# The start of an SSD layer: the first batch's norm made in place and in skewed stages, the first front beside it, and two kinds of stores on ScalarE's queue

## The chip, the cores and the metric

The kernel runs on one core of a Trainium2 chip. The metric is device time in microseconds for one execution of the whole program. Engines are named as in the profile: PE (TensorE; PEld are its weight loads), DVE (VectorE), ACT (ScalarE), POOL (GpSimd), and SP (SyncE), which issues DMAs.

## What is computed

Four layers follow each other on an image batch of 4 x 96 x 64 x 64 in f32: a selective-scan layer with a fusion and a batch norm, a state-space layer with scalar decays (the "SSD" layer), the first kind again, and a ConvNeXt block. The change touches the second layer alone. Cut to what matters, with L = 64 x 64 tokens, 3 heads of 64, 128 states:

```python
residual = x                                   # [4, 96, L]
xn = rmsnorm over the 96 channels of x, times norm_w
xs = xn in four orders: rows, rows reversed, columns, columns reversed
z, xBC, dt = split(xs @ in_proj_w.T)           # 192, 192 + 2 * 128, 3 columns
dt = softplus(dt + dt_bias)
xBC = silu(causal convolution of xBC over 4 tokens + conv_b)
y = ssd(x, dt, -exp(A_log), B, C) + D * x      # within chunks and from chunk to chunk
y = rmsnorm(y * silu(z)) @ out_proj_w.T
out = mean of the four orders, put back in place, + residual
```

The layer's x is not stored by the layer before. That layer leaves its raw output (raw), its residual (res) and the scale and shift of its batch norm (bn), which are known only when its last token is done. So the SSD layer first makes x = raw * scale + shift + res, "the sum".

## The kernel before

Class Ssd holds the layer. A batch is 96 channels by 4096 tokens. Three sizes of pieces occur: chunks of T = 512 tokens (NT = 8) in the preparation, blocks of BLK = 1024 tokens in the front, and chunks of Q = 128 tokens in the recurrence, eight (QB) to a block. There are 64 steps, (batch b, order o, direction r, block), four blocks to a direction; o = 0 is by rows, o = 1 by columns, r = 1 reversed.

For each direction there is a prelude (line 763 on). For r = 0 it makes the normalised tokens and the step sizes, for both directions the decays:

- rmsnorm(b) (line 665): for each of the 8 chunks, loads raw and res into the tiles nx and nr (two buffers each), applies the batch norm on ACT (line 673), adds res on DVE (674), stores the sum to DRAM from SP's queue (675), squares on ACT (677), takes the mean over channels by a matmul with a constant matrix (679), makes the inverse root by Ln and Exp on ACT (the helper at line 107), and writes xn[0] on DVE (682).
- turn() (line 684) copies xn[0] into xn[1] by columns, on POOL, for o = 1.
- step_sizes(o) (line 696): for each chunk a matmul into a bank "front" (706), a copy on ACT to a row tile dtrow (711, which shares the two buffers of nsq), a store of it to DRAM from SP's queue (712); then one load of all rows in another layout (717), the softplus on ACT, DVE and POOL, and a transpose on PE (725).
- decays(r) (line 729): cumulative sums by matmuls with triangles (743, 745), exponentials, a transpose (756), and a store of the sums (760), which the steps load again as dr (850), broadcast to all partitions.

weights_of (line 616) loads the layer's weights: inw (620), the convolution's weights conv (624), which DVE multiplies with inw (626) and seven DMAs spread into sconv (629); xbias, bcbias (631, 633); ad (638), of which ACT makes a; the output weights opw and gn (656, 657), multiplied on DVE (659).

front(b, o, r, blk) (line 781) prepares one block: six DMAs stack shifted tokens into pk (777); z by matmuls (796, r = 0 only); B and C by 12 matmuls of pk with sconv (814); x by 24 (825); then one silu over all of it on ACT, which needs another table set (line 112), and transposes of B (842). decay, weights, outputs, scale, by_channels and finish then work on the 128-token chunks, spread over the loop in run() with lags, while front makes the next block and a prelude, taken one step per chunk, the next direction. finish adds the outputs into X (973), a tile that holds the batch's whole sum; switch(b) (line 975) stores X when a batch is done and loads the next batch's sum from DRAM into it (983).

All matmuls of preludes and front go through PSUM banks with the tag "front", of which there are two.

What sets the order: the Python code writes one program, and a planner at build time distributes it over the engines' queues. The place in the program is an instruction's rank; an instruction that is ready by the planner's own durations may go ahead of older ones that are not. The trace shows this: POOL's copies of turn() for o = 1 stand at 3077.30 us, between the chunks of the first norm. Once placed, an engine's queue runs strictly in order, SP's queue of DMAs too. All DMAs of the kernel are issued by SP.

The start of the layer is written out in run():

```python
first = preludes.pop(0)[1]
for _ in range(2):
    next(first)
self.weights_of(self.w)
for _ in first:
    pass
self.switch(0)
for _ in front(0):
    pass
```

That is: two chunks of the first norm, all weights, the rest of the first prelude, the load of X, the first front; then the loop over chunks.

Of the kernel before, what the change touches and what calls it, by code (L numbers as in the profile page):

```python
# [18 lines left out]
F32 = mybir.dt.float32  # L19
AF = mybir.ActivationFunctionType  # L20
ALU = mybir.AluOpType
# [4 lines left out]
B, C, HH, WW = 4, 96, 64, 64  # L26
L = HH * WW
P = 128
T = 512
NT = L // T  # L30
# [27 lines left out]
DI = 192  # L58
DST = 128
NH = 3  # L60
HD = 64
CONV = DI + 2 * DST
# [4 lines left out]
PAD = 3  # L67
# [55 lines left out]
def rsqrt(act, out, in_, eps):  # L123

    act.exp_ln(out, in_, AF.Ln, bias=eps)
    act.exp_ln(out, out, AF.Exp, scale=-0.5)
# [446 lines left out]
class Ssd:  # L573
# [42 lines left out]
    def weights_of(self, w):  # L616

        nc, k, one = self.nc, self.k, self.one
        self.inw = one.tile([C + 1, 2 * DI + 2 * DST + NH], F32, name="inw")
        nc.sync.dma_start(self.inw, w["in"])  # L620

        conv = self.work.tile([P, 3 * BLK], F32, tag="pk", name="conv")
        conv = conv[:C, : 4 * CONV].rearrange("c (k n) -> c k n", k=4)
        nc.sync.dma_start(conv, w["conv_wT"].partition_broadcast(C))
        xbc = self.inw[:C, DI : DI + CONV]
        nc.vector.tensor_tensor(conv, conv, xbc[:, None].to_broadcast([C, 4, CONV]), ALU.mult)
        self.conv = one.tile([P, 3, CONV], F32, name="sconv")
        for i, r0, r1, tap, c0 in PIECES:
            nc.sync.dma_start(self.conv[r0:r1, i], conv[c0 : c0 + r1 - r0, tap])
        self.xbias = one.tile([P, DI], F32, name="xbias")  # L630
        nc.sync.dma_start(self.xbias, w["in"][C, DI : 2 * DI].partition_broadcast(P))
        self.bcbias = one.tile([P, 2], F32, name="bcbias")
        nc.sync.dma_start(
            self.bcbias, w["in"][C, 2 * DI : 2 * DI + 2 * DST].rearrange("(q p) -> p q", q=2)
        )

        self.ad = one.tile([P, 2, NH], F32, name="ad")
        nc.sync.dma_start(self.ad, w["ad"].partition_broadcast(P))
        self.a = one.tile([P, 1, NH], F32, name="a")
        k.act.exp_ln(self.a[:, 0], self.ad[:, 0], AF.Exp)  # L640
        nc.vector.tensor_scalar_mul(self.a, self.a, -1.0)

        self.opw = one.tile([P, 4, C], F32, name="opw")
        gn = one.tile([P, 4], F32, name="gn")
        nc.vector.memset(self.opw, 0.0)
        nc.vector.memset(gn, 0.0)  # L650
        low, up = slice(0, HD), slice(HD, P)
        for j, rows, n, of in (
            (0, slice(0, P), slice(0, P), 0), (1, low, low, 1), (2, up, low, 0), (3, low, up, 0),
            (3, up, up, 2),
        ):
            nc.sync.dma_start(self.opw[rows, j], w["out"][n, of])
            nc.sync.dma_start(gn[rows, j : j + 1], w["gnorm"][n, of : of + 1])
        for j in range(4):
            nc.vector.tensor_scalar(
                self.opw[:, j], self.opw[:, j], gn[:, j : j + 1], 0.25, ALU.mult, ALU.mult  # L660
            )

    def bank(self, tag):
        return self.psum.tile([P, T], F32, tag=tag, name=tag, bufs=2)

    def rmsnorm(self, b):
        nc, k = self.nc, self.k
        for c in range(NT):
            t = ds(c * T, T)
            x, res = (self.work.tile([C, T], F32, name=n) for n in ("nx", "nr"))  # L670
            nc.sync.dma_start(x, self.raw[b, :, t])
            nc.sync.dma_start(res, self.res[b, :, t])
            nc.scalar.activation(x, x, AF.Identity, bias=self.bn[1], scale=self.bn[0])
            nc.vector.tensor_tensor(x, x, res, ALU.add)
            nc.sync.dma_start(self.src[b, :, t], x)
            sq = self.work.tile([C, T], F32, name="nsq")
            nc.scalar.activation(sq, x, AF.Square)
            pv = self.bank("front")[:C]
            nc.tensor.matmul(pv, lhsT=k.mean, rhs=sq, start=True, stop=True)
            rsqrt(k.act, sq, pv, self.eps)  # L680
            xn = self.xn[0][:C, ds(PAD + c * T, T)]
            nc.vector.scalar_tensor_tensor(xn, x, self.norm, sq, ALU.mult, ALU.mult)
            yield

    def turn(self):
# [7 lines left out]
            )  # L693
            yield

    def step_sizes(self, o):

        nc, k = self.nc, self.k
        n = NQ * NH
        rows = self.dram.tile([NH, L], F32, name="dtrows")
        for c in range(NT):
            pd = self.bank("front")[:NH]
            nc.tensor.matmul(
                pd, lhsT=self.inw[:, DI + CONV :], rhs=self.xn[o][:, ds(PAD + c * T, T)],
                start=True, stop=True,
            )
            row = self.work.tile([C, T], F32, tag="nsq", name="dtrow")[:NH]  # L710
            nc.scalar.copy(row, pd)
            nc.sync.dma_start(rows[:, ds(c * T, T)], row)
            yield
        x, ua, lg = (
            self.work.tile([n, Q], F32, tag=m, name=m, bufs=1) for m in ("dtx", "ua", "row")
        )
        nc.sync.dma_start(x, rows.rearrange("h (c t) -> c h t", t=Q))
        yield
        nc.scalar.activation(ua, x, AF.Abs)
        nc.vector.tensor_scalar_max(x, x, 0.0)  # L720
        lo = self.work.tile([C, T], F32, tag="nsq", name="lo")[:n, :Q]
        softplus_tail(nc, k.act, x, ua, lg, lo)
        yield
        pt = self.bank("front")[:, :n]
        nc.tensor.transpose(pt, x, k.ident[:n, :n])
        self.dt = self.work.tile([P, n], F32, name="dt")
        nc.vector.tensor_copy(self.dt, pt)
# [35 lines left out]
    def prelude(self, b, o, r):  # L763

        if r == 0:
            yield from self.rmsnorm(b) if o == 0 else self.turn()
            yield from self.step_sizes(o)
        self.seq[b, o, r] = self.decays(r)

    def stack(self, o, r, blk):  # L770
# [9 lines left out]
    def front(self, b, o, r, blk, made, following):  # L780
# [2 lines left out]


        nc, k = self.nc, self.k
        made.update(self.seq[b, o, r])
        xn = self.xn[o]
        base = blk * BLK
        pk = self.stack(o, r, blk) if self.pk is None else self.pk
# [1 line left out]
        if r == 0:  # L791
            z = self.z[blk] = self.work.tile([P, QB, DI], F32, name="z", bufs=L // BLK + 1)
            for c in range(0, QB, 2):
                p = self.bank("front")[:, : 2 * DI]
                for i in range(2):
                    nc.tensor.matmul(
                        p[:, i * DI : (i + 1) * DI],
                        lhsT=xn[:C, ds(PAD + base + (c + i) * Q, Q)], rhs=self.inw[:C, :DI],
                        start=True, stop=True,
# [8 lines left out]
        x = made["x"] = pre[:, :n1].rearrange("p (c n) -> p c n", c=QB)  # L808
# [177 lines left out]
    def run(self):  # L986
# [16 lines left out]
        def front(n):  # L1003
            if n >= len(steps):
                return iter(())
            return self.front(*steps[n], made[n], steps[n + 1] if n + 1 < len(steps) else None)
# [3 lines left out]
            (n, self.prelude(*steps[n][:3])) for n in range(0, len(steps), nblk)  # L1010
        ]
        first = preludes.pop(0)[1]
        for _ in range(2):
            next(first)
        self.weights_of(self.w)
        for _ in first:
            pass
        self.switch(0)
        for _ in front(0):
            pass  # L1020
        for n in range(-4, len(chunks) + 4):
            def at(lag):
# [289 lines left out]
```

## Time and profile before

| | |
|---|---|
| median of 3 runs | 9949.42 us (9938.72 to 9961.11) |
| the profiled execution | 9940.69 us |
| its span | 9939.0 us |
| busy: PE, DVE, ACT, POOL | 8555.7, 8200.3, 5528.2, 6968.8 us |
| first load of the sum's parts, SSD layer | 3066.55 us |
| first silu's table load in it | 3170.66 us |
| last add into X (line 973) | 6182.87 us |

A row of the order of time reads: start and length in us, engine, line of the kernel, operation, the tile written and the tiles read, how many, and in brackets how long the engine stood idle before it and what ended that. "SPq" is an instruction in SP's queue; its length is that of the issue, and the transfer lands later. Busy time of an engine does not say that it bounds anything; in a start-up stretch in which the engines take turns, all of them are idle most of the time.

### The profile page before, as it was taken

The page shows a single profiled execution, that of the slowest core. Times are in us where ns is not written, and L with a number is a line of the kernel's source. Part 1 is how long each engine was busy: PE and PEld are TensorE (multiplying, and loading weights), DVE is VectorE, ACT ScalarE, POOL GpSimd, SP SyncE. Part 2 cuts the span into 40 slices and gives each one's busy share as a digit, 9 for nine tenths or more (in the row PEclk, how much of TensorE's full clock was granted, in tenths as well). Part 3 has the DMA queues.
Part 4 walks back from the last instruction along what each step waited for, and adds up shares of the span by engine and source line. Part 5 has one row for each costly group of instructions (what it writes and reads, how often), then busy time and mean ns, then how long its engine had stood idle before and what let it go on. Part 6 is the DMA issues. An engine that isn't in the chain of part 4 may idle for free. (4 is left out here: it accounts for less than half of the span.)

```text
span 9939.0 us, 109693 instructions
## 1 busy us (share of the span) xinstructions
PE 8555.7 (86%) x32744; PEld 3519.5 (35%) x32744; DVE 8200.3 (83%) x10861; ACT 5528.2 (56%) x10500; POOL 6968.8 (70%) x4600
## 2 busy tenths in 40 slices
PE   7888888888886998998998988788888888888688
PEld 1222212222212676776776776122222222211122
DVE  7999999999995666666666666799999999999787
ACT  5666666566663455555455554566666665665244
POOL 6888888888884555555555555688888888888322
PEclk8999999999997999999999998899999999999798
DMA  7677677677674223222222222767777777776432
GB/s 189 199 204 202 201 207 206 196 205 208 198 206 121 66 71 92 72 69 83 79 74 74 82 67 57 194 199 205 211 204 206 206 203 200 208 203 199 113 97 74
DMA packets 803535, 1528.27 MB, mean 154 GB/s; under 512 B 124253, under 2 KB 128249, under 8 KB 802170
## 3 DMA queue, kind: packets, MB, share of 16 engines
q1 hardware_dynamic: 802938, 1521.25, 54.4%
q8 instruction: 260, 4.26, 0.2%
q14 instruction: 337, 2.76, 0.1%
HBM read 1229.69 MB, written 156.37 MB: 139 GB/s over the span
## 5 line engine op out<-in xcount | busy, mean ns | idle before, releaser
L342 POOL TENSOR_TENSOR hc<-hs,bc 128x1024 f32<-128x1024 f32 x1536 | 3608.0, 2356 | 630.3 <-DVE hs L340 550.9
L340 DVE TENSOR_TENSOR_SCAN hs<-da,carry,bs 128x512 f32<-128x512 f32 x2016 | 2467.0, 1265 | 81.1 <-DVE bs L335 2.7
L107 ACT ACTIVATE da<-da,w_a 128x512 f32<-128x512 f32 x2304 | 1617.2, 716 | 1273.2 <-DMA da<-dd 1229.1
L361 PE MATMUL py<-hc,selsum 128*32 128x512 f32 x6144 | 1797.4, 637 | 469.8 <-POOL hc L342 463.4
L313 PE MATMUL bs<-du,seldu 64*128 64x512 f32 x4608 | 1570.6, 676 | 208.8 <-DVE hs L340 193.0
L335 DVE TENSOR_TENSOR bs<-bs,bc 128x1024 f32<-128x1024 f32 x1152 | 1398.4, 1214 | 180.2 <-PE bs L313 177.3
L308 POOL TENSOR_TENSOR du<-du,bc 128x1024 f32<-128x1024 f32 x384 | 904.7, 2356 | 279.8 <-DMA du<-dg 144.0
L361 PEld LDWEIGHTS py<-hc,selsum 128*32 128x32 f32 x6144 | 239.3, 110 | 1814.3 <-POOL hc L342 1125.4
L879 POOL TENSOR_TENSOR seg<-seg,cb 128x384 f32<-128x384 f32 x512 | 514.8, 1007 | 516.9 <-DVE cb L878 434.0
L863 DVE TENSOR_SCALAR seg<-dr,dac 128x128 f32<-128x128 f32 x1536 | 645.6, 454 | 276.3 <-PE y L908 269.1
L313 PEld LDWEIGHTS bs<-du,seldu 64*128 64x128 f32 x4608 | 445.6, 195 | 1202.6 <-DVE hs L340 857.0
L194 PE MATMUL pu<-h,w_conv 96*128 96x512 f32 (+3 forms) x2048 | 835.3, 628 | 11.7 <-ACT rs L107 11.6
L340 DVE TENSOR_TENSOR_SCAN hs<-bs,carry,du 128x512 f32<-128x512 f32 x672 | 823.6, 1260 | 6.7 <-issue 5.1
L814 PE MATMUL front<-pk,sconv 128*128 128x512 f32 x1536 | 756.7, 610 | 24.5 <-ACT z L802 20.4
L918 POOL TENSOR_TENSOR y<-y,xs 128x192 f32<-128x192 f32 x496 | 294.4, 594 | 626.0 <-DVE y L917 619.7
L931 ACT ACTIVATE y<-yz 128x192 f32<-128x192 f32 x512 | 186.1, 364 | 903.5 <-DVE yz L930 902.5
L883 POOL TENSOR_TENSOR xs<-pre,coef 128x576 f32<-128x576 f32 x512 | 597.1, 1171 | 65.6 <-ACT pre L112 32.4
L825 PE MATMUL front<-sconv,pk 128*128 128x192 f32 x3072 | 572.8, 329 | 51.1 <-DVE pre L830 46.0
L1175 DVE SCALAR_TENSOR_TENSOR acc<-pad,c_conv,acc 96x1024 f32<-96x1024 f32 x336 | 491.8, 1467 | 110.5 <-ACT acc L1166 59.2
L345 ACT COPY carry<-hs 128x2 f32<-128x2 f32 x1344 | 250.7, 187 | 569.7 <-DVE hs L340 566.1
L825 PEld LDWEIGHTS front<-sconv,pk 128*128 128x128 f32 x3072 | 496.5, 190 | 81.8 <-DVE pre L830 72.3
L107 ACT ACTIVATE bs<-da,w_a 128x512 f32<-128x512 f32 x768 | 522.0, 680 | 2.2 <-DMA da<-dd 0.7
(196 smaller groups left out, 13878.7 us busy)
## 6 DMA issues: line engine op xcount, KB each, us to landing
da<-dd SPq DMA_DIRECT2D x3072, 256.0 KB
du<-dg SPq DMA_DIRECT2D x768, 256.0 KB
dr<-rows SPq DMA_DIRECT2D x256, 384.0 KB
bc<-rows SPq DMA_DIRECT2D x256, 256.0 KB
dd<-delta SPq DMA_DIRECT2D x192, 256.0 KB
dg<-du SPq DMA_DIRECT2D x192, 256.0 KB
pk<-xn SPq DMA_DIRECT2D x128, 384.0 KB
pk<-xn SPq DMA_DIRECT2D x128, 256.0 KB
```

Source lines behind the costliest of these rows:

```text
L107: self.last = self.scalar.activation(out, in_, func, **kw)
L194: nc.tensor.matmul(pu[r0:r1], lhsT=wt["conv"][:kk, tap, d0:d1], rhs=h[:kk, b, ds(tap, T)], start=(tap == 0), stop=(tap == 3),)
L308: nc.gpsimd.tensor_tensor(g["du"], g["du"], self.b_or_c(g, 0), ALU.mult)
L313: nc.tensor.matmul(g["bs"][:, i], lhsT=self.sel["du"][rows, g["half"], g["q"]], rhs=g["made"]["du"][rows, g["j"]], start=True, stop=True,)
L335: nc.vector.tensor_tensor(dbx, dbx, self.b_or_c(g, 0), ALU.mult)
L340: nc.vector.tensor_tensor_scan(hs[:, i], da[:, i], dbx[:, i], init, ALU.mult, ALU.add)
L342: nc.gpsimd.tensor_tensor(g["hc"], hs, self.b_or_c(g, 1), ALU.mult)
L361: nc.tensor.matmul(py[rows], lhsT=self.sel["sum"][:, g["q"]], rhs=g["hc"][:, i], start=(g["q"] == 0), stop=(g["q"] == NQU - 1),)
L814: nc.tensor.matmul(p, lhsT=self.conv[:, i, DI + q * DST : DI + (q + 1) * DST], rhs=pk[:, i, ds(c * T, T)], start=(i == 0), stop=(i == 2),)
L825: nc.tensor.matmul(p, lhsT=pk[:, i, ds(c * Q, Q)], rhs=self.conv[:, i, :DI], start=(i == 0), stop=(i == 2),)
L863: nc.vector.tensor_scalar(seg[:, h], g["pair"]["dr"][:, c % 2 * NH + h], made["dac"][:, n0 + h : n0 + h + 1], 0.0, ALU.subtract, ALU.min,)
L883: nc.gpsimd.tensor_tensor(xs, x.to_broadcast([P, 3, NH, HD]), coef.to_broadcast([P, 3, NH, HD]), ALU.mult)
```

## The change

weights_of becomes a generator with three parts: the loads of inw and conv; the multiplied convolution weights, biases and a; the output weights. The first batch no longer goes through rmsnorm but through a new function, begin(). It loads raw straight into X and res into xn[1], which is free until turn(); two chunks ahead of the first part of the weights, six behind it. Then it makes the sum in X itself, so that neither the store of the sum nor the reload of X is needed for batch 0, and works in stages that are skewed against each other: in turn n the chunk n is summed and squared, n - 1 gets its mean and inverse root, n - 2 its normalised tokens, n - 3 its matmul for the step sizes, and n - 4 its row and the row's store. The squares use the buffers nx and nr by turns. After begin() comes the second part of the weights, then the first front, in which every third step is followed by a step of what is left of the prelude (the load of the rows, the softplus, the transpose and the decays); the output weights come last.

For the other batches rmsnorm loads a chunk one step ahead of its work, and stores the sum from ScalarE's queue, behind the square. The rows of step sizes are stored from ScalarE's queue in all preludes. The diff, without comments and the unchanged rest:

```diff
@@ weights_of
         nc.sync.dma_start(conv, w["conv_wT"].partition_broadcast(C))
+        yield
...
         nc.vector.tensor_scalar_mul(self.a, self.a, -1.0)
+        yield
@@
+    def begin(self):
+        nc, k = self.nc, self.k
+        rest = self.xn[1][:C]
+        for c in range(NT):
+            nc.sync.dma_start(self.X[:, ds(c * T, T)], self.raw[0, :, ds(c * T, T)])
+            nc.sync.dma_start(rest[:, ds(PAD + c * T, T)], self.res[0, :, ds(c * T, T)])
+            if c == 1:
+                yield
+        self.batch = 0
+        rows = self.dram.tile([NH, L], F32, name="dtrows")
+        sq, pd = {}, {}
+        for n in range(NT + 4):
+            if 0 <= (c := n - 4):
+                row = self.work.tile([C, T], F32, tag="nsq", name="dtrow")[:NH]
+                nc.scalar.copy(row, pd.pop(c))
+                nc.scalar.dma_start(rows[:, ds(c * T, T)], row)
+            if n < NT:
+                x = self.X[:, ds(n * T, T)]
+                nc.scalar.activation(x, x, AF.Identity, bias=self.bn[1], scale=self.bn[0])
+                nc.vector.tensor_tensor(x, x, rest[:, ds(PAD + n * T, T)], ALU.add)
+                sq[n] = self.work.tile([C, T], F32, tag=("nx", "nr")[n % 2], name="sq")
+                nc.scalar.activation(sq[n], x, AF.Square)
+            if 0 <= (c := n - 1) < NT:
+                pv = self.bank("front")[:C]
+                nc.tensor.matmul(pv, lhsT=k.mean, rhs=sq[c], start=True, stop=True)
+                rsqrt(k.act, sq[c], pv, self.eps)
+            if 0 <= (c := n - 2) < NT:
+                xn = self.xn[0][:C, ds(PAD + c * T, T)]
+                nc.vector.scalar_tensor_tensor(
+                    xn, self.X[:, ds(c * T, T)], self.norm, sq.pop(c), ALU.mult, ALU.mult
+                )
+            if 0 <= (c := n - 3) < NT:
+                pd[c] = self.step_rows(0, c)
+        return rows
@@ rmsnorm
-        for c in range(NT):
-            t = ds(c * T, T)
-            x, res = (self.work.tile([C, T], F32, name=n) for n in ("nx", "nr"))
-            nc.sync.dma_start(x, self.raw[b, :, t])
-            nc.sync.dma_start(res, self.res[b, :, t])
-            nc.scalar.activation(x, x, AF.Identity, bias=self.bn[1], scale=self.bn[0])
-            nc.vector.tensor_tensor(x, x, res, ALU.add)
-            nc.sync.dma_start(self.src[b, :, t], x)
-            sq = self.work.tile([C, T], F32, name="nsq")
-            nc.scalar.activation(sq, x, AF.Square)
...
+        loaded = []
+        for c in range(NT + 1):
+            if loaded:
+                n, x, res = loaded.pop()
+                nc.scalar.activation(x, x, AF.Identity, bias=self.bn[1], scale=self.bn[0])
+                nc.vector.tensor_tensor(x, x, res, ALU.add)
+                sq = self.work.tile([C, T], F32, name="nsq")
+                nc.scalar.activation(sq, x, AF.Square)
+                nc.scalar.dma_start(self.src[b, :, ds(n * T, T)], x)
...
+            if c < NT:
+                x, res = (self.work.tile([C, T], F32, name=n) for n in ("nx", "nr"))
+                nc.sync.dma_start(x, self.raw[b, :, ds(c * T, T)])
+                nc.sync.dma_start(res, self.res[b, :, ds(c * T, T)])
+                loaded.append((c, x, res))
             yield
@@ step_sizes (the matmul alone is now step_rows; rows may be given)
-            row = self.work.tile([C, T], F32, tag="nsq", name="dtrow")[:NH]
-            nc.scalar.copy(row, pd)
-            nc.sync.dma_start(rows[:, ds(c * T, T)], row)
-            yield
+        if rows is None:
+            rows = self.dram.tile([NH, L], F32, name="dtrows")
+            for c in range(NT):
+                row = self.work.tile([C, T], F32, tag="nsq", name="dtrow")[:NH]
+                nc.scalar.copy(row, self.step_rows(o, c))
+                nc.scalar.dma_start(rows[:, ds(c * T, T)], row)
+                yield
@@ prelude
-            yield from self.rmsnorm(b) if o == 0 else self.turn()
-            yield from self.step_sizes(o)
+            if (b, o) == (0, 0):
+                rows = yield from self.begin()
+                yield
+            else:
+                rows = None
+                yield from self.rmsnorm(b) if o == 0 else self.turn()
+            yield from self.step_sizes(o, rows)
@@ run
-        for _ in range(2):
-            next(first)
-        self.weights_of(self.w)
+        weights = self.weights_of(self.w)
+        next(first)
+        next(weights)
+        next(first)
+        next(weights)
+        for m, _ in enumerate(front(0)):
+            if m % 3 == 2:
+                next(first, None)
         for _ in first:
             pass
-        self.switch(0)
-        for _ in front(0):
+        made[0].update(self.seq[steps[0][:3]])
+        for _ in weights:
             pass
```

## The prediction

> **What bounds the kernel now.** I read the page's busy lines first: they mix four layers and say little about an edit that touches one place. So I went to the order of time around the start of the SSD layer, then to the busy table by stretch, then to the waits, last the waits of SP's own queue. The chain on the page covers only the last layer, so the chain of the start has to be put together from the instructions.
>
> Start of the SSD layer in order of time (start us, length us, engine, line, operation; in brackets the idle time before and what ended it):
>
> ```profile
> 3069.65 0.29 SPq L620 DMA_DIRECT2D inw<-in_L_in  x1
> ...
> 3070.80 0.81 ACT L673 ACTIVATE nx<-nx,bn 96x512 f32<-96x512 f32 x1 [5.49 <-DMA nx<-raw]
> ...
> 3086.62 2.02 DVE L626 TENSOR_TENSOR conv<-conv,inw 96x1792 f32<-96x1792 f32 x1 [9.39 <-DMA conv<-in_L_conv_wT]
> ...
> 3097.02 0.53 SPq L671 DMA_DIRECT2D nx<-raw  x1
> ...
> 3100.05 0.81 ACT L673 ACTIVATE nx<-nx,bn 96x512 f32<-96x512 f32 x1 [12.16 <-DMA nx<-raw]
> ...
> 3140.87 0.31 ACT L719 ACTIVATE ua<-dtx 96x128 f32<-96x128 f32 x1 [4.18 <-DMA dtx<-dtrows]
> ...
> 3146.81 5.20 PE L796 MATMUL front<-inw,xn 96*128 96x192 f32 x16 [0.45 <-DVE row L758]
> ```
>
> The same start by stretch (length, then busy us of PE, PEld, DVE, ACT, POOL, then the granted clock, DMA share, GB/s):
>
> ```profile
> 3078.00:3098.00 20.00, 0.00 (x0) 0.00 (x0) 4.39 (x7) 0.74 (x2) 1.40 (x2) 0.50 0.24 61
> 3098.00:3137.00 39.00, 21.85 (x28) 3.71 (x28) 8.88 (x13) 20.70 (x32) 6.32 (x6) 0.58 0.65 192
> 3137.00:3147.00 10.00, 2.28 (x7) 1.45 (x8) 3.03 (x12) 3.04 (x8) 0.90 (x2) 0.55 0.61 174
> 3147.00:3171.00 24.00, 23.19 (x88) 17.05 (x88) 6.24 (x22) 5.31 (x11) 0.00 (x0) 0.90 0.42 131
> ```
>
> The reader is to see four pieces in a row from 3066 to the first silu (its table load is at 3170.66): two chunks normalised by 3078; 20 us in which nearly nothing runs; the other six chunks and the eight rows of step sizes, 39 us; the chain rows, softplus, decays, 10 us; the first front, 24 us, the only piece in which PE is full. Nothing overlaps. What this start costs, the whole layer is later.
>
> The hole: SP's queue stood in order behind the weights. The reload of chunk 2 (L671) was issued only at 3097.02. Waits of SP's queue (total us, times, longest) in 3066 to 3147:
>
> ```profile
> SPq L712 <- ACT dtrow L711: 8.2, 8, 3.5
> SPq L671 <- DVE xn L682: 5.7, 4, 1.8
> SPq L657 <- DMA inw<-in_L_in: 5.1, 1, 5.1
> ```
>
> The load gn (L657), eight DMAs after inw, waits for inw to land: inw took from 3069.65 to 3084.47, 14.8 us for 243.6 KB, while the load of chunk 0, 192 KB, needed 4.25 us (3066.55 to 3070.80). In 3082 to 3086 the DMA share is 0.08 and 26 GB/s: about one engine of sixteen at work. What was issued behind inw did not land before it: conv at 3086.6, ad at 3087.69 (ACT stood 9.15 us for it).
>
> **The change at the start.** Removed for batch 0: eight stores of the sums (L675), four reloads of X (L983), the two-buffer limit on the loads. Neither stores nor reloads are on the path above (the last reload is issued at 3130.41, the first add to X comes after 3200), so their removal alone is 0. Moved: the six other chunk loads go ahead of the weights' later DMAs; the first front goes beside the chain of step sizes.
>
> Step 1, when chunk 2 lands. Its load is now issued at about 3074, but behind inw and conv. Everything behind inw landed at 3086.6 to 3087.7 before; I take 3088. Bounds: 3078.5 if a load behind inw is not held (3074 + 4.25), 3092 if twelve loads queue up on the same engine before it. I take 3088 because conv and ad are rows of just this queue. After that a chunk's two loads add 24 KB to each engine's share, at inw's 16.5 KB/us 1.5 us; SP waits again at the eighth DMA after inw, which is chunk 5's, and that wait ends with inw too. So loads come faster than ACT takes them.
>
> The Trainium skill, page "DMA: Bandwidth & Descriptors", section "Why a DMA increments its semaphore by 16 and not by 1", has the rule behind that row: the number of engines is the largest one up to 16 that divides the slowest dimension of both sides, so that a prime number of rows goes to a single engine. inw has 97 rows, and 0.08 is near 1/16. By that rule the change, which leaves inw ahead of twelve loads, can't get chunk 2 before inw ends; if it did not hold here, the sum would be some 9.5 us better.
>
> Step 2, ACT then sets the pace. Per chunk: 0.81 (L673) + 0.63 (L677) + 0.68 + 0.63 (L107 twice) + 0.57 (L711) = 3.32 us, and the issue of the row's store, which now is ACT's; SP needed 0.24 for it (L712). 3.56 x 6 = 21.4. Of chunks 0 and 1, idle time before 3088 takes the first two steps; say 3.5 us of their rest is left over. 3088 + 21.4 + 3.5 = 3113 for the last row. DVE (0.69 + 0.75 per chunk, conv's 2.02 once) and PE (L679 2.02, L706 1.5) fit beside it.
>
> Step 3, the front. Before it took 3146.81 to 3170.2, 23.4 us, PE full. Its inputs: sconv, which needs conv's multiplication (after 3086.6 as before) and seven issues (4.4 us), and pk's six (3.4 us) behind those, xbias, bcbias and ad (3.9 us): about 3106. But its matmuls use the same two "front" banks as the norm and the rows, and come later in the program, which the planner takes as rank. So I let the front begin at 3113 and take 23.4 us, with 2.5 us more for the transposes and decays now put between (PE 2.28 us in 3137 to 3147): silu at 3139. Bounds: full overlap from 3106 gives 3106 + 23.4 - some 5 of z done earlier = 3125; none, and the chain of 10 us ahead of it as now, 3147.
>
> Where the decays go: rows at 3113, plus 10.7 (3136.1 to 3146.8 as now) = 3124, plus dr's landing (3146.78 to 3154.60, 7.8 us) = 3132, before silu. So the 10 us are hidden under the front; if PE meets the transposes too early, it stalls for what is missing of them, which is inside the bounds. Late next is PE's front itself.
>
> Sum of the start: 3170.7 - 3139 = 32 us gained (24 to 46).
>
> **The change in the rest.** 56 rows (seven of eight preludes, the first counted above) and 24 stores of sums go from SP to ACT: 80 issues. No DMA of ACT stands in this trace. Nearest rows: SP's 0.24 (L712) and 0.30 us (L675), 80 x 0.27 = 22 us of ACT at most, if all of it shows; below, nothing, as ACT is busy only half of these stretches and the store of the sums falls where ACT waits for the mean anyway. Queued behind such an issue are the exponentials of seg, for which POOL, then PE, wait. I take a quarter, 5 us. On the other side SP's queue is relieved, but hardly anybody waits for it: over the whole layer DVE waited 6.8 us for dr, all at the start, and ACT for nx 1.4 us in the fourth quarter of batch 0; times three, 4 us. Ends: 22 lost, 4 gained.
>
> **Sum.** -32 + 5 = -27 us. The profiled execution took 9940.7 us (span 9939.0), which gives 9913.7; the median of the runs, 9949.4, lies 8.7 us above it, and the runs spread over 22 us. The same difference taken from the median: 9922.
>
> **Rivals.**
> Given back at the start (0.21). ACT meets the load of ad again, as in its 9.15 us wait, or the front's pk is late behind SP's waits, and silu comes at 3150 to 3155: 16 to 20 us gained, less 5. Net 11 to 15: 9936. For: in this trace the planner put ACT's a<-ad into the middle of the norm, and its DMA is as slow as inw lets it be. Against: ad's load now stands behind all chunk loads, where ACT has older work.
>
> Better (0.10). Loads are not held by inw and z is done early: silu at 3125, 46 us gained, nothing lost after: 9903.
>
> Slower (0.11). An ACT-issued store must also wait for the DMA eight places before it, as gn did for inw; if that is a dr load which SP has not issued yet, ACT stands. SP waits on average 8.0 us for dr's buffer (L850 <- DVE y L919: 1153.4 us in 144 times) and 15 at worst. It would have to take back 32 us and 20 more: 52 / 8.0, seven of the 80 issues. Result from 9969 up. For: that mechanism is in the trace. Against: a step of 45 us has ten DMAs without a prelude, so the eighth before lies over 25 us back, longer than SP's longest wait.
>
> **How the numbers follow.** Forecast 0.58, given back 0.21, better 0.10, slower 0.11. 0.2%, 20 us, is about what a measurement can tell from no change. Forecast and better lie beyond it: faster 0.68; given back: within, 0.21; slower 0.11. The range reaches from the better case taken off the profiled execution, 9940.7 - 46 = 9895, to about no change, 9948; outside are the slower rival and the tails, under 2 in 10.
>
> **What will show it.** Right: chunk 2's first ACT instruction near 3088, no hole of 20 us; the last row near 3113; the front's PE time beside dtx, softplus and decays; the first silu at 3135 to 3145; the later spacing of the steps as before within 1%. Wrong: chunk 2 at 3078; silu after 3150; ACT idle in front of a DMA issue in the later steps. An order of the planner that differs in every step of the layer, by 1 us in 64 steps, would break the sum either way.

## The result, and the profile after

The changed kernel takes 9939.1 us (median of 12 runs, 9926.45 to 9965.25); beside it the kernel before took 9941.2 (12 runs, 9922.02 to 9961.11). The ratio is 0.9999, 95% interval [0.9990, 1.0009]. A second measurement of the same code gave 0.9987 [0.9975, 0.9999]. By the two ratios the change is worth 1 and 13 us, and neither measurement tells it clearly from nothing. The forecast was a gain of 27. The time lies in the range given, but in the case called "within 0.2%", not in the one called likeliest.

The profiled execution took 9941.65 us (span 9939.6), before 9940.69 (span 9939.0). The whole span cut at five marks shows where time went. The start runs from the aggregate of the batch statistics (L556) to the first silu of the SSD layer, the steps from the first to the last silu of the 64 steps:

| stretch | before, us | after, us | difference |
|---|---|---|---|
| layers one and two, to L556 | 3063.7 | 3057.4 | -6.3 |
| start of the SSD layer | 108.2 | 88.1 | -20.1 |
| 63 steps | 2962.3 | 2974.5 | +12.2 |
| last step to the layer's end | 48.6 | 48.9 | +0.3 |
| third layer, same code | 3062.0 | 3074.6 | +12.6 |
| fourth layer and rest, same code | 694.1 | 696.1 | +2.0 |

The start did get shorter, by 20 us instead of 32. Two stretches took it back, and one of these contains no changed instruction. (The first two layers, unchanged as well, were 6.3 us shorter; the runs do not say why.) This is the third layer by stretch (length, busy us and count of PE, PEld, DVE, ACT, POOL, granted clock, DMA share, GB/s), first in the kernel before:

```profile
6183.00:9245.00 3062.00, 2610.51 (x7944) 608.00 (x7944) 2792.71 (x2585) 1842.73 (x3295) 2537.64 (x1222) 0.94 0.71 200
```

and in the changed one:

```profile
6169.00:9243.50 3074.50, 2645.18 (x7944) 613.55 (x7944) 2793.43 (x2585) 1843.66 (x3295) 2537.93 (x1222) 0.93 0.71 199
```

The counts are equal to the instruction; DVE, ACT and POOL are busy equally long to 1.1 us. Only PE is 35 us longer, at a clock of 0.93 instead of 0.94: it stood at half rate for 433 us here and for 348 us before. A single pair of profiles can therefore differ by over 10 us without any cause in the edit, and each stretch has to be read with its clock beside it.

Now the start, in order of time in the changed kernel (start us, length us, engine, line, operation; in brackets the idle time before and what ended it):

```profile
3061.91 0.28 SPq L620 DMA_DIRECT2D inw<-in_L_in  x1
...
3063.11 0.81 ACT L688 ACTIVATE X<-X,bn 96x512 f32<-96x512 f32 x1 [4.14 <-DMA X<-raw]
...
3079.26 2.02 DVE L627 TENSOR_TENSOR conv<-conv,inw 96x1792 f32<-96x1792 f32 x1 [9.59 <-DMA conv<-in_L_conv_wT]
...
3079.76 0.81 ACT L688 ACTIVATE X<-X,bn 96x512 f32<-96x512 f32 x1 [9.52 <-DMA X<-raw]
...
3090.09 2.02 PE L694 MATMUL front<-sq,mean 96*96 96x512 f32 x2
...
3092.05 1.87 PE L743 MATMUL front<-xn,inw 97*3 97x512 f32 x2
...
3110.20 1.65 PE L850 MATMUL front<-inw,xn 96*128 96x192 f32 x4
...
3112.26 0.57 ACT L684 COPY dtrow<-front 3x512 f32<-3x512 f32 x1
...
3133.20 8.03 PE L879 MATMUL front<-sconv,pk 128*128 128x192 f32 x48
...
3142.18 0.81 ACT L712 ACTIVATE nx<-nx,bn 96x512 f32<-96x512 f32 x1 [8.09 <-DMA nx<-raw]
3143.03 0.69 DVE L713 TENSOR_TENSOR nx<-nx,nr 96x512 f32<-96x512 f32 x1 [2.37 <-ACT nx L712]
3143.64 0.35 DVE L884 TENSOR_TENSOR pre<-front,xbias 128x192 f32<-128x192 f32 x1
...
3144.21 1.28 ACT L112 ACT_TABLE_LOAD   x1 [1.22 <-DVE pre L884]
```

The end of the front in the kernel before:

```profile
3162.15 8.03 PE L825 MATMUL front<-sconv,pk 128*128 128x192 f32 x48
...
3170.66 1.28 ACT L112 ACT_TABLE_LOAD   x1 [7.62 <-DVE pre L830]
```

The start of the changed kernel by stretch, columns as above:

```profile
3060.00:3070.00 10.00, 4.04 (x4) 0.79 (x4) 2.48 (x5) 4.53 (x7) 7.40 (x4) 0.50 0.82 205
3070.00:3079.70 9.70, 0.00 (x0) 0.00 (x0) 0.44 (x1) 0.24 (x1) 0.00 (x0) 0.50 0.33 102
3079.70:3113.00 33.30, 28.37 (x34) 4.95 (x35) 13.14 (x16) 20.45 (x35) 8.01 (x8) 0.50 0.49 136
3113.00:3126.00 13.00, 11.54 (x30) 6.87 (x28) 1.99 (x10) 4.29 (x11) 0.90 (x2) 0.75 0.21 53
3126.00:3144.20 18.20, 14.90 (x60) 10.68 (x60) 7.33 (x28) 2.54 (x5) 0.00 (x0) 0.88 0.63 205
```

The reader is to see five things. The hole of 20 us has become one of 9.5 us, and conv and chunk 2 end it within half a microsecond of each other: both stood behind inw. From there to the last row PE is busy 28.4 of 33.3 us and ACT 20.5, so PE is the fuller engine. The clock there is 0.50. And the front (first z matmul at 3110.20) does begin before the last row is copied, but the silu comes 31.4 us after that copy. Last, 3.0 of these lie behind PE's last matmul of the front, which ends at 3141.23 (in the kernel before: 0.5): the last piece of pre (L884) stands in DVE's order behind an add for batch 1's first chunk (L713), and that waits for a load.

Times from the first chunk's load (3066.55 before, 3060.05 after) put prediction and outcome side by side:

| mark | before | predicted | after |
|---|---|---|---|
| ACT begins chunk 2 | 33.5 | 21.5 | 19.7 |
| last row copied | 70.1 | 46.5 | 52.8 |
| table load of the first silu | 104.1 | 72.5 | 84.2 |

### The profile page after: what moved, and what is told of

Its sections match the earlier page's. It is cut to its first block, busy times and chain, and to the rows that moved or that the text cites. A ratio compares the mean times of both kernels' runs of the same rounds, so it can differ in the third digit from the quotient of the medians.

```text
span 9939.6 us, 109594 instructions
## 1 busy us (share of the span) xinstructions
PE 8611.3 (87%) x32744; PEld 3540.4 (36%) x32744; DVE 8210.0 (83%) x10861; ACT 5526.8 (56%) x10500; POOL 6972.6 (70%) x4600
## 5 line engine op out<-in xcount | busy, mean ns | idle before, releaser
L313 PE MATMUL bs<-du,seldu 64*128 64x512 f32 x4608 | 1593.3, 684 | 208.7 <-DVE hs L340 196.1
L985 ACT ACTIVATE y<-yz 128x192 f32<-128x192 f32 x512 | 186.1, 363 | 914.1 <-DVE yz L984 913.4
```

Of the source, the lines that this page charges most:

```text
L313: nc.tensor.matmul(g["bs"][:, i], lhsT=self.sel["du"][rows, g["half"], g["q"]], rhs=g["made"]["du"][rows, g["j"]], start=True, stop=True,)
```

## The experiments

Three theories stood at first for the steps, where some of the gain went. **A**: each of the 80 issues costs ScalarE time. **B**: only the clock differs. **C**: the new order in the later norms (each chunk finished a turn after its load) costs. **D**, **E** and **F** came later, out of the runs: the last row's store stands late in ACT's order (D); any DMA put into ACT's order costs by its place there (E); what costs is the way of the rows from PE to the decays, which goes through those stores (F).

All runs in one table. The ratio is to the kernel before; start and steps as in the table above; "half" is how long the granted clock was 0.5 during the steps. The last column sums, over the seven later preludes, the time from the end of the copy of the last row (dtrow) to DVE's copy of dt, the transposed step sizes. "All on SP" means that all three `nc.scalar.dma_start` of the change are `nc.sync.dma_start` again.

| kernel | ratio [95%] | start | steps | half | last row to dt, x7 |
|---|---|---|---|---|---|
| before | 1 | 108.2 | 2962.3 | 273 | 100.4 |
| after | 0.9999 [0.9990, 1.0009] | 88.1 | 2974.5 | 295 | 105.8 |
| e5, after again | 0.9987 [0.9975, 0.9999] | 88.4 | 2980.4 | 280 | 109.5 |
| e1, all on SP | 0.9970 [0.9956, 0.9984] | 82.4 | 2958.6 | 249 | 102.7 |
| e2, queue alone | 1.0003 [0.9990, 1.0015] | 112.6 | 2962.2 | 225 | 102.8 |
| e3, start alone | 0.9975 [0.9963, 0.9987] | 82.3 | 2962.5 | 273 | 101.6 |
| e4, inw in two loads | 0.9984 [0.9972, 0.9997] | 73.9 | 2973.8 | 282 | 104.9 |
| e6, all on SP, inw in two | 0.9959 [0.9944, 0.9974] | 76.1 | 2949.7 | 232 | 101.3 |
| e11, e6 again | 0.9956 [0.9945, 0.9968] | 76.3 | 2959.9 | 239 | 104.5 |
| e7, stores doubled | 0.9992 [0.9979, 1.0005] | 86.2 | 2976.9 | 280 | 114.6 |
| e8, start's rows on SP | 0.9989 [0.9978, 1.0001] | 82.1 | 2989.3 | 335 | 110.3 |
| e9, last rows on SP | 0.9989 [0.9977, 1.0001] | 88.2 | 2981.9 | 317 | 110.9 |
| e10, sums on SP | 0.9981 [0.9970, 0.9991] | 87.6 | 2967.0 | 251 | 106.1 |
| e12, spare rows on ScalarE | 0.9971 [0.9959, 0.9982] | 82.8 | 2943.2 | 212 | 99.5 |

A straight-line fit over the fourteen profiles gives 0.25 us of steps per us of half clock; at equal clock, kernels whose rows go through ScalarE to their reader are 10.6 us longer (standard error 2.3), and those with the new order of the later norms 0.2 shorter (2.4).

**The two halves of the change (e1, e2, e3).** e1 is the change with all stores on SP:

```diff
-                nc.scalar.dma_start(rows[:, ds(c * T, T)], row)
+                nc.sync.dma_start(rows[:, ds(c * T, T)], row)
...
-                nc.scalar.dma_start(self.src[b, :, ds(n * T, T)], x)
+                nc.sync.dma_start(self.src[b, :, ds(n * T, T)], x)
...
-                nc.scalar.dma_start(rows[:, ds(c * T, T)], row)
+                nc.sync.dma_start(rows[:, ds(c * T, T)], row)
```

> The changed kernel with all three kinds of stores back on SP's queue; nothing else. The changed kernel's profile has the start 20.1 us shorter (from the batch norm's aggregate to the first silu 88.1 us against 108.2), and the 63 steps that follow 12 us longer, while the times are the same as before. Theory A (ScalarE's issues take the gain back in the steps): start 88 +- 2 us, whole 0.998, 20 us under before. Theory B (the start's gain is real but is paid back by TensorE's clock, whatever queue stores): start 88, whole within 8 us of before. Theory C (the reordered norm of batches 1 to 3 takes it back): 8 us under before, no more.

e2 is the kernel before, with only the stores moved:

```diff
             nc.vector.tensor_tensor(x, x, res, ALU.add)
-            nc.sync.dma_start(self.src[b, :, t], x)
             sq = self.work.tile([C, T], F32, name="nsq")
             nc.scalar.activation(sq, x, AF.Square)
+            nc.scalar.dma_start(self.src[b, :, t], x)
...
-            nc.sync.dma_start(rows[:, ds(c * T, T)], row)
+            nc.scalar.dma_start(rows[:, ds(c * T, T)], row)
```

> The kernel before with only the stores of the sums and of the rows moved to ScalarE's queue (the store of the sums behind the square, as in the change). Theory A: 10 to 14 us slower than before, 1.0010 to 1.0014, with the steps of the preludes (fifth to eighth and thirteenth to sixteenth of a batch) each longer. Theory B and C: within 4 us of before; start 108 +- 2 us.

e3 has the new start (`begin`, the weights in parts, the front between) over the old `rmsnorm`, and all stores on SP.

> The kernel before with only the new start: the first batch's norm in X in skewed stages, the first front beside the rest of the prelude, the weights in three parts; norm of batches 1 to 3 as before, all stores on SP's queue. Theory A and C: start 88 us, 20 us under before, 0.998. Theory B: within 8 us of before although the start is 20 us shorter.

e1 gains 30 us [16, 44] and e3 25 [13, 37]. They differ only in the order of the later norms, so theory C falls; the start alone, with SP's stores, is worth 26 us by the profile. e2 gives nothing, 1.0003, though its profile had 48 us less of half clock in the steps than before: at the slope of 0.25 it should have been 12 us shorter there, and it was 2962.2 against 2962.3. Theory B alone does not explain that. Its start is 112.6, 4.4 us longer than before. So the new start gains, and the move to ScalarE's queue takes back most of it.

The start itself is 6 us shorter on SP, which was not expected: 88 us had been said for both. In the changed kernel SP waited in 3057 to 3146 (total us, times, longest) for

```profile
SPq L766 <- DMA dtrows<-dtrow: 10.2, 3, 4.5
SPq L831 <- DMA dtrows<-dtrow: 7.8, 3, 3.8
...
SPq L674 <- DMA inw<-in_L_in: 6.2, 1, 6.2
```

and in e1, over 3059 to 3142, for

```profile
SPq L685 <- ACT dtrow L684: 19.2, 8, 4.4
...
SPq L674 <- DMA inw<-in_L_in: 6.2, 1, 6.2
```

With the stores on ScalarE, SP stands in front of the loads of dtx (L766) and of pk (L831) until rows have landed; on SP it waits for the copies instead, and no wait for the landing is listed. e1's clock also rose earlier, as its start by stretch shows:

```profile
3082.00:3113.00 31.00, 27.52 (x37) 4.75 (x38) 12.58 (x16) 20.31 (x35) 8.60 (x8) 0.54 0.33 87
3113.00:3125.00 12.00, 8.56 (x27) 3.86 (x25) 2.27 (x11) 4.24 (x11) 0.90 (x2) 0.97 0.58 158
3125.00:3140.20 15.20, 14.55 (x60) 10.52 (x60) 5.21 (x23) 1.70 (x4) 0.00 (x0) 0.91 0.53 152
```

In 3113 to 3125 e1 has 0.97 where the changed kernel has 0.75 in about the same piece. Between the copy of the last row and the silu's table load PE is busy 23.5 us in e1 and 26.6 in the changed kernel: 3.1 us that go with the clock. Another 2.4 are DVE's order: behind PE's last matmul e1 has 0.55 us to the table load, the changed kernel 2.97. All six kernels with the new start and its rows on ScalarE have 2.3 to 4.4 us there, the six with the new start and its rows on SP (e1, e3, e6, e8, e11, e12) 0.5 to 0.8.

**The start's eight rows back on SP (e8).**

```diff
@@ begin
-                nc.scalar.dma_start(rows[:, ds(c * T, T)], row)
+                nc.sync.dma_start(rows[:, ds(c * T, T)], row)
```

> The changed kernel with only the first batch's eight row stores back on SP's queue; the other 80 stay on ScalarE's. Theory A: start 82.4 us as with all on SP, steps from first to last silu 2970 to 2976 us, whole 5 to 6 us under the changed kernel of this set and some 10 over all-on-SP (9907 us). If the loss sits in the start's eight issues alone, this is as fast as all-on-SP.

The start is 82.1, as in e1: moving these eight stores alone costs the start 6 us, with the planner's order and the clock that came with the move. The ratio, 0.9989, is 4 us under the mean of the changed kernel's two (0.9993); with its interval it can't tell 6 us from nothing. This profile's steps, 2989.3, had 335 us of half clock, the most of all; at a half clock of 270 us, by the slope of 0.25, they are 2973.3, as in the changed kernel.

**Issue time (e7).** Each store of the change in the later preludes once more, to a place that nobody reads:

```diff
+        twin = self.dram.tile([C, L], F32, name="twin")
...
+                nc.scalar.dma_start(twin[:, ds(n * T, T)], x)
...
+            spare = self.dram.tile([NH, L], F32, name="spare")
...
+                nc.scalar.dma_start(spare[:, ds(c * T, T)], row)
```

> The changed kernel with each of the 80 stores on ScalarE's queue in the later preludes issued twice, the second to a place that nobody reads; the start as in the change. Theory A, each issue holds ScalarE: another 10 to 16 us over the changed kernel of this set, the idle time of ACT behind the copies of the rows up by some 20 us again. Theory B (the clock, not the issues): no more than 4 us over it.

Twice the issues gave 0.9992 and steps of 2976.9, or 2974.4 if that slope brings them to a half clock of 270 us; the changed kernel's two profiles give 2968.3 and 2977.9 there, 2973.1 in the mean. So 80 more issues cost about 1 us, where the two profiles of one code differ by 10 and theory A asked for 10 to 16 more. Theory A falls, and with it the prediction's bound of 22 us from ScalarE's time.

**Which of the stores (e9, e10).** In e9 the last row of each later prelude goes by SP, in e10 the sums do:

```diff
@@ step_sizes (e9)
-                nc.scalar.dma_start(rows[:, ds(c * T, T)], row)
+                (nc.sync if c == NT - 1 else nc.scalar).dma_start(rows[:, ds(c * T, T)], row)
@@ rmsnorm (e10)
-                nc.scalar.dma_start(self.src[b, :, ds(n * T, T)], x)
+                nc.sync.dma_start(self.src[b, :, ds(n * T, T)], x)
```

> The changed kernel with only the last of the eight rows of each later prelude stored from SP's queue; the other seven, the sums and the start stay as in the change. At an equal clock the ScalarE kernels need 11.6 +- 2.2 us more from first to last silu than the SP kernels, and twice the issues (e7) cost nearly nothing more. Theory D: the price is the place of the last row's store in ACT's in-order queue; the planner put it behind a square that waits for DVE, so it is issued 4.7 us after its copy, and the load of all rows, the softplus and the decays follow. Then here: rows loaded 3.5 us or less after the last copy instead of 6.1, the columns' first silu 77 to 78.5 us after the last copy instead of 79.5 to 81, steps 5 to 9 us shorter at an equal clock, whole 5 to 9 us under the changed kernel. Theory A (each issue holds ACT): one eighth less, 1 to 2 us.

> The changed kernel with the stores of the sums of batches 1 to 3 back on SP's queue; all rows stay on ScalarE's. Theory D and A-for-rows: within 3 us of the changed kernel. If the sums' stores were the price: 11 us less from first to last silu at an equal clock, and 11 less in all.

e9: 0.9989, and 110.9 us from the last row to dt, no shorter than after; theory D would have brought that back to 101. e10: 0.9981; its steps at equal clock, 2971.8, and its 106.1 us are those of the changed kernel (mean 2973.1; 105.8 and 109.5). The sums are not the price; the rows are.

**Place in ACT's order, or the rows' way (e12).** e1, in which each later row is stored from ScalarE too, into a spare tile that nobody reads:

```diff
+            spare = self.dram.tile([NH, L], F32, name="spare")
             for c in range(NT):
...
                 nc.sync.dma_start(rows[:, ds(c * T, T)], row)
+                nc.scalar.dma_start(spare[:, ds(c * T, T)], row)
```

> All stores that are read again on SP's queue, as in the all-on-SP kernel, and besides each row of the later preludes stored once more from ScalarE's queue to a place that nobody reads. Not the number of issues (twice cost 1 us), not the sums (nothing), and only some 2 us of the last row's place explain the 10 us that the kernels with rows on ScalarE's queue lose in the steps at an equal clock, 270 us at half: 2968 to 2978 us against 2959 to 2967. Theory E (the issue's place in ACT's order, with what the planner puts around it): 2970 to 2976 us, idle time of ACT behind the copies 139 to 147 us as in all kernels with rows on ScalarE. Theory F (the rows' way to the decays, late because of ACT's queue): 2959 to 2967 us, idle time 112 to 124 us, whole as all-on-SP, 0.9965 to 0.9975.

0.9971 [0.9959, 0.9982], as e1. The sum of ACT's idle times behind the copies of rows, all 64 of the layer, is 142 us, as in kernels with the rows on ScalarE (137 to 148; on SP 112 to 124, which had been expected here if F holds), but it costs nothing: the row-to-dt sum is 99.5, and the steps, at equal clock, are the shortest of all. Theory E falls. F stands in this: the price comes only with stores that are read again. How the two queues treat the last row is seen in one prelude, in the changed kernel:

```profile
4193.30 0.57 ACT L760 COPY dtrow<-front 3x512 f32<-3x512 f32 x1 [0.22 <-PE front L743]
...
4198.50 0.36 ACT L985 ACTIVATE y<-yz 128x192 f32<-128x192 f32 x1 [4.63 <-DVE yz L984]
4198.57 0.24 ACTq L761 DMA_DIRECT2D dtrows<-dtrow  x1
...
4199.93 0.57 SPq L766 DMA_DIRECT2D dtx<-dtrows  x1
...
```

and at the same place in e12:

```profile
4201.01 0.57 ACT L761 COPY dtrow<-front 3x512 f32<-3x512 f32 x1
...
4203.90 0.25 SPq L762 DMA_DIRECT2D dtrows<-dtrow  x1
...
4206.22 0.24 ACTq L763 DMA_DIRECT2D spare<-dtrow  x1
...
4206.50 0.58 SPq L768 DMA_DIRECT2D dtx<-dtrows  x1
...
```

ScalarE issues the store 4.7 us after the copy's end, once the square of a gated output (L985), ahead of it in ACT's order, had got its input from DVE; e12's spare store does the same (4206.22, 4.6 us), while SP had sent the real one 2.3 us after the copy. The loads of dtx then come 6.1 and 4.9 us after it. In this prelude the loads come 1.1 us later; the table's last column has the sums over seven. SP's wait for the landing of rows in the steps, changed kernel and then e12:

```profile
SPq L766 <- DMA dtrows<-dtrow: 29.9, 7, 5.1
```

```profile
SPq L768 <- DMA dtrows<-dtrow: 12.0, 7, 2.3
```

The rows' way on ScalarE gives 102.8 to 114.6 us in the eight kernels that have it, 99.5 to 104.5 in the six that have not: in the mean 108.1 against 101.7. That is 6 of the 10.6 us of the fit in the mean, but not kernel by kernel: e2 has 102.8, 2.4 more than before, and at equal clock its steps are 12 us longer than before's (2973.3 against 2961.5).

Where in the steps the price lies can be read from the times between the silus. In seven of the 63 intervals the last rows of a later prelude are copied, loaded again and made into dt. These seven sum up to 348.5 to 364.2 us in the eight kernels with the rows on ScalarE and to 336.4 to 346.8 in the six others. By the same kind of fit, without the term for the new order, 7.9 us (error 1.1) of the 10.6 lie there and 2.5 (1.4) in the other 56 intervals; the seven just before, in which the first four or five rows are copied, have none (-1.2, error 2.1). So the price stands where the rows are read, not wherever one is issued.

**The hold of inw (e4, e6, e11).** The load of inw as 96 rows and 1 row, in the changed kernel (e4) and in e1 (e6, and e11 once more):

```diff
-        nc.sync.dma_start(self.inw, w["in"])
+        nc.sync.dma_start(self.inw[:C], w["in"][:C])
+        nc.sync.dma_start(self.inw[C:], w["in"][C:])
```

> The changed kernel with inw loaded in two pieces, 96 rows and the bias row, so that no DMA of 97 rows stands ahead of the chunk loads. If the 97 rows are what holds chunk 2: first ACT instruction of chunk 2 some 5 to 8 us after that of chunk 0 instead of 16.6, start 78 to 80 us instead of 88, whole 8 to 10 us under the changed kernel. If loads are held by something else (the wait at the eighth DMA, HBM), start 86 to 88 and no change.

> The changed kernel with all stores on SP's queue and inw in two pieces, 96 rows and one. Inw in two took 14 us off the start on the ScalarE version (73.9 us against 88.1), SP's queue 6. If both add up: start 68 to 70 us, whole 36 to 44 us under before, 0.9956 to 0.9964. If the start is then bound by the same ACT pace and front either way: start 74 us, 0.9968.

e4, order of time:

```profile
3067.51 0.41 SPq L675 DMA_DIRECT2D X<-raw  x1
...
3069.37 0.42 SPq L620 DMA_DIRECT2D inw<-in_L_in  x1
3069.84 0.28 SPq L621 DMA_DIRECT2D inw<-in_L_in  x1
...
3078.58 0.81 ACT L689 ACTIVATE X<-X,bn 96x512 f32<-96x512 f32 x1 [0.19 <-DMA X<-raw]
...
3137.42 1.28 ACT L112 ACT_TABLE_LOAD   x1 [4.48 <-DVE pre L885]
```

ACT begins chunk 2 after 11.1 us from the first load instead of 19.7, and its wait for it, 9.52 us, is down to 0.19. The start is 73.9 (78 to 80 had been expected), 14.2 less than after. That is the condition of the rival "better" ("loads are not held by inw"), which the change itself did not meet. Only 8.6 of the 14.2 us are chunk 2's. From there to the last row e4 needs 2.9 us less (30.2, not 33.1), and behind the last row 28.6 us at a clock of 0.93, the changed kernel 31.4 at 0.83. With the stores on SP as well it gives 0.9959 and a start of 76.1, neither the 68 to 70 nor the 74 expected: against e1 chunk 2 comes 9.5 us sooner, but from the last row to the table load it takes 30.4 us at 0.80 instead of 27.5 at 0.94. So the hold is worth some 9 us in both; what follows it, at a higher clock in e4 and a lower one in e6, makes 14 or 6 of them. Measured once more

> All stores on SP's queue and inw in two pieces once more, since it had six runs: 0.9959 with 0.9944 to 0.9974. Should come inside that interval, 0.9950 to 0.9968; start 76 us. If its higher clock (0.939 against 0.936) was chance, 0.9968 to 0.9978.

0.9956 [0.9945, 0.9968]: 44 us under the kernel before, the best version here and the only kind that lies clear of 0.2% in both its measurements.

**The change once more (e5).** It has no edit.

> The changed kernel once more, beside the others of this set. The new start alone and all stores on SP's queue were 0.9975 and 0.997 of before, the changed kernel 0.9999: ScalarE's queue should then be worth 25 to 29 us, but moved alone it was 1.0003. If ScalarE's queue costs 10 to 16 us whatever the start (theory A), this comes at 0.9985 to 0.9995 here, start 88 us, the steps from first to last silu 2970 to 2976 us. If the 0.9999 was made by the clock of those runs alone (theory B), 0.997 to 0.998.

0.9987 [0.9975, 0.9999], start 88.4, steps 2980.4 at 280 us of half clock. Start and steps repeat; the ratio moved by 0.0012, which is half the width of its interval.

## Where the prediction was right and where it failed, step by step

The time fell into the range, but the gain forecast, 27 us, did not come: the start gained less and the steps lost more than said. That the two stayed inside a range of 53 us is no proof of the sum.

**The hole (step 1) was right.** Chunk 2 came at +19.7 where +21.5 was said, held by inw as the conv and ad rows of before had indicated, and e4 shows that it was inw: two loads, and the hold is gone. (The prediction's list of SP's waits leaves out its longest line, that of the stores of the sums, which the change removes for batch 0; the reading of inw stands without it.)

```profile
SPq L675 <- DVE nx L674: 15.5, 9, 3.9
```

The rule on 97 rows, from the Trainium skill, page "DMA: Bandwidth & Descriptors", section "Why a DMA increments its semaphore by 16 and not by 1", agrees with e4: a split into 96 rows and 1 was enough.

**Step 2, "ACT then sets the pace", failed.** I added ACT's instructions, 3.56 us per chunk, and let PE fit beside them with 2.02 (L679) and 1.5 (L706). Both matmuls are PE's: 3.52 already by these numbers, as much as ACT. The row's takes 1.87 at the clock of 0.50 that this piece has: 3.9 us per chunk, more than ACT's sum. The trace shows the pair alternating, 2.02 and 1.87, back to back, from 3082.60 to 3101.40. The last row came at +52.8 instead of +46.5, 6.3 us later, and from chunk 2 on it took 33.1 us instead of 25.0. Some 2 us of that are ACT's order: PE's last matmul for a row ended at 3110.27, and ACT copied z ahead of that row (3112.26).

**Step 3, the length of the front, failed by 5.4 us.** From the last row to the silu I took 26 us (23.4 of before, plus 2.5), all of them PE's work, and it took 31.4. PE was busy 26.6 of these and idle 4.8, and I had put the idle time at nothing. 3.0 us of it lie behind PE's last matmul, where the silu waits for DVE (L884 behind L713); the other 1.8 stand around the transposes and the matmuls of the decays. The clock cost as well: the 23.4 had been measured at 0.90; here PE ran at 0.75 in 3113 to 3126 and 0.88 behind that, and with the 1.65 us of z done ahead of the last row the work took 28.3 us instead of 25.9. The early z gave most of that back. In e1, with 0.97 and 0.91 in the two pieces and 0.55 us behind PE's last matmul, the silu came 78.4 us after the first load. Together the two steps make 11.7 of the 12 us by which the start's gain fell short (32 said, 20 measured).

The Trainium skill, page "TensorE: Matmul & The Clock Gate", section "Part 1: The HAM clock gate (the "warmup" mystery)", lets the clock rise after a busy window of some 3.4 us. The trace differs: PE was busy 28.4 of 33.3 us by its records, without a gap from 3082.60 to 3101.40, and the clock stayed at 0.50 all the while. The measurement decides; what would have raised the clock here is not known.

**The rest, 5 us, was too small and had the wrong mechanism.** I priced the move of 80 stores as issue time on ScalarE, 22 us at most, a quarter of it taken. e7 shows that issue time costs about 1 us per 80. The price is 10.6 us (error 2.3) in the steps and 6 more at the start (e8, with its clock and order), and it comes with the rows that are read again: the store waits in ACT's order, and the dependent loads on SP wait for it to land. That the store has a reader was not weighed: the text asked what is queued behind the issue on ScalarE, and not who waits for the stored rows. That rival's cover ("hardly anybody waits" for SP's queue) was right for SP and no help: SP's order had been good for these stores.

**The sum.** Start -20, steps +10.6: some -10 us, at the edge of the first interval ([-10, +9] us) and inside the second ([-25, -1]). The rival "given back" named 16 to 20 us gained at the start, less 5; its 9936 is near the result, but its causes (the load of ad, pk behind SP's waits) were only in part those found: SP did wait 7.8 us in front of pk, for rows, by the profile.

**What stays open.** The two profiles of before and after differ by 12.6 us in the third layer alone, by the clock. The versions with the new start and the rows on SP ran at mean clocks of 0.9370 to 0.9392 over their timed runs, those with the rows on ScalarE at 0.9346 to 0.9380, and within a kernel's runs 0.001 of clock goes with some 5 us. So about 10 us of the distance between the two kinds may be clock. Whether the queue causes that, or it is chance of few kernels, no run settles. What speaks against mere chance is that most of the price stands in seven intervals. Open too is how much of the rows' price is the late store and how much the wait for the landing: e9 took SP's wait for the rows down to 11.0 us (after: 29.9) and did not shorten the way to dt. Nor is PE's own wait for the input of dt the price by itself: over the seven preludes it is 4.1 to 7.9 us in seven of the ScalarE kernels and 0 to 1.2 in five of the six others, but 1.7 in e9, which pays the price, and 3.4 in e12, which does not. The planner's order changes with every edit, as the late L884 at the start shows; that rival was not tested apart from the queue. No kernel was tried that leaves the rows on ScalarE at an earlier place in its order.

## What to carry to other kernels

Before a store is moved to another engine's queue, ask who reads what it writes: here the price came with the stores that have a reader, and 80 more issues without one cost about 1 us. When work is pulled forward, price it at the clock of the place to which it goes, and add up every engine's instructions for one round of the loop before one of them is called the pace. A stretch of unchanged code, read in both profiles, tells how much of a difference is only the clock.

## What was not expected of the hardware

One load of 97 rows held what was issued behind it on its queue (conv and chunk 2 landed within 0.5 us of each other, after a hole of 9.5): as 96 rows and 1 it shortened the start by 14.2 us (88.1 to 73.9) in the changed kernel and by 6.2 (82.4 to 76.2) in the version on SP, with chunk 2 some 9 us sooner in both. The granted clock falls to a half in episodes of 3.4, 6.8, 10.2 or 13.7 us and more, all through the kernel, for 12 to 14% of the time in the fourteen profiles; in the steps a microsecond of it costs 0.25 us by the fit, and in the third layer, with identical code, 84 us more of it went with 12.6 us.
